# Moving the norm products of a windowed-attention layer from the head of a turn's seventh step to the tail of its sixth

## The chip, the cores and the metric

The kernel runs on one core of a Trainium2 chip. A core has five engines with an instruction queue each: TensorE (PE, matrix products; PEld is its weight load), VectorE (DVE), ScalarE (ACT), GpSimd (POOL) and SyncE (SP, which starts DMAs). The metric is the device time of one execution in microseconds (us), measured from outside the program; the median of several executions is given with the lowest and highest. A profile is one execution recorded by the hardware, and its span can differ from the median by a few microseconds.

## The reference

The program is four layers, one after the other, on two images of 512 channels and 64 x 64 pixels, each layer added to its input after a group norm. The change is in the first layer only, a local attention with a 3 x 3 window and 256 pooled keys:

```python
q = (xf @ W_q + b_q).reshape(B, N, nh, hd).transpose(0, 2, 1, 3)
q_norm = _l2norm(q)
q_scaled = (q_norm + query_embedding[None]) * jax.nn.softplus(temperature)[None]
kv = xf @ W_kv + b_kv
k_l, v_l = (kv[..., :C], kv[..., C:])
k_l = _l2norm(k_l.reshape(B, N, nh, hd)).reshape(B, N, C)
# ... 3 x 3 patches of k_l and v_l, scores against them and against 256 pooled keys,
# ... one softmax over all, and the weighted sums of the values
lt = jnp.einsum('bhnd,hdk->bhnk', q_norm, learnable_tokens) + learnable_bias[None] + a_local
x_local = jnp.einsum('bhnk,bhndk->bhnd', lt, v_local)
x_pool = jnp.einsum('bhnp,bhpd->bhnd', a_pool, v_pool)
out = ((x_local + x_pool).transpose(0, 2, 1, 3).reshape(B, N, C) @ W_proj + b_proj)
```

`_l2norm` divides each head's 64 channels of every pixel by their norm. The change moves the instructions that do this division.

## The kernel before

The first layer works in turns. Each turn handles one unit of 128 channels and 1024 pixels (16 units an image), and several units are in flight at different stages. A stage is a Python generator: it records some instructions, yields, and goes on at its next step. `in_turn` takes one step of every stage in the order of the list, then the next step of every stage, until all have ended:

```python
def in_turn(*gens):
    gens = list(gens)
    while gens:
        gens = [g for g in gens if next(g, gens) is not gens]
```

The turns of an image (`units` is 16; `i` runs over 21 values):

```python
for i in range(-4, units + 1):
    k, q, ahead, u, before = (unit(i + n) for n in (4, 3, 1, 0, -1))
    streams = []
    stages = [self.norms(streams)]
    if before is not None:
        stages.append(self.weigh(before))
    if ahead is not None:
        stages.append(self.tap_products(ahead))
    if u is not None:
        stages.append(self.attend(u))
    if ahead is not None:
        stages.append(self.tap_sums(ahead))
    stages.append(self.projections(k, q, ahead, streams))
    if i < -2:
        stages.append(islice(heads, 12 if i == -4 else None))
    if i == units - 3:
        stages.append(self.fetch_output())
    if i > units - 3:
        stages.append(self.output(i - units + 2))
    in_turn(*stages)
```

`projections` fills `streams` with up to four pieces of raw keys and queries of 512 pixels each; the next turn's `norms` normalises them. Its steps, with numbers added here as comments:

```python
def norms(self, streams):
    before, self.pending = self.pending, streams
    if not before:
        return
    yield                                        # 1: nothing
    ps = self.bank()                             # 2: sums of squares, copied out
    for s in range(4):
        nc.tensor.matmul(ps[32 * s:32 * s + 32, :], self.cst[:, C_E32:C_E32 + 32],
                         before[s % len(before)][4], start=True, stop=True)
    rows = wp.tile([P, TB], F32, name="n_rows")
    nc.scalar.copy(rows, ps)
    yield
    # ... 3: transposed, max with 1e-24 into n; yield
    # ... 4: POOL takes n to the power -1/2, into self.wide; yield
    # ... 5: nothing; yield
    ps = self.bank()                             # 6: transposed back
    for t in range(NT):
        nc.tensor.transpose(ps[:, t * P:(t + 1) * P], self.wide[:, t, :], self.net.ident)
    rows = wp.tile([P, TB], F32, name="n_rows")
    nc.scalar.copy(rows, ps)
    yield
    banks = [self.bank() for _ in before]        # 7: the products
    for s, ps in enumerate(banks):
        nc.tensor.matmul(ps, self.cst[32 * s:32 * s + 2, C_ROW:C_ROW + P],
                         rows[32 * s:32 * s + 2, :], start=True, stop=True)
    for (which, u, j, part, _), ps in zip(before, banks):
        # ... out is the place in kx for a key, part itself for a query
        nc.vector.tensor_tensor(out, part, ps, ALU.mult)
    yield
    if before[-1][0] == "q":                     # 8
        self.learned(before[-1][1])
    yield
```

The other stages at the steps that matter: `weigh` records instructions at its steps 2, 3, 5, 7, 9, 10 and 11 (steps 3, 5, 7 and 9 weigh two of the nine window positions of the values each; step 6 is empty); `tap_products` one DVE product at each of its first nine steps; `attend` the second half's product with the values (`values(1)`) at step 6; `tap_sums` products at steps 3, 5, 7, 9 and 10 and nothing at step 6; `projections` a projection of values at steps 1, 4, 7 and 10, and those of keys and queries at steps 7 to 10, so nothing at step 6. `attend`'s `values`:

```python
def values(j):
    psO = self.bank()
    for k2 in range(2):
        for h, c in enumerate(heads):
            nc.tensor.matmul(psO[c, :], self.vp[:, k2, cc * P + h * HD:][:, :HD],
                             prob[j, k2][h], start=(k2 == 0), stop=(k2 == 1))
    nc.scalar.copy(out[:, j * TB:(j + 1) * TB], psO)
    # ... two sums of prob on POOL
```

`self.bank()` is the next of five PSUM buffers, in rotation, shared by all these stages; the tap products and sums have a buffer apiece of their own.

Of the kernel before, what the change touches and what calls it, by code (L numbers as in the profile page):

```python
# [49 lines left out]
# [6 lines that stand above are left out]
# [872 lines left out]
class Net(General):  # L928
# [361 lines left out]
    def key_context(self, X, Y, d, nmean, rstd, mv, row2, queries, kp, wp, pp):  # L1290
# [19 lines left out]
        def prepare(blk):  # L1310
            ks, sqs = wp.tile([P, KC, TB], F32, name="k"), []
            yield from self.projected_squares(X, wk, bk, blk, ks, sqs, wp, pp)
            if blk == NB - 1:
                queries.wq = self.load3(d, "Wq3")
            ed = wp.tile([P, NT, NH], F32, name="ed")
            va = lent[blk % 2].rearrange("p (t h c) -> p t h c", t=NT, h=NH)
            norms = self.half_norm_columns(sqs, e2h, wp, pp)
            for t in range(NT):
                if t:
                    cols = next(norms)  # L1320
                    if t == 2:
                        nc.scalar.mul(ed.rearrange("p t (c h) -> p t c h", h=2), cols, -1.0)
                lo = blk * TB + t * P
                ps = pp.tile([P, TB], F32, name="mm")
                for kc in range(KC):
                    nc.tensor.matmul(ps, X[:, kc, lo:lo + P], wv[:, kc, :], start=(kc == 0),  # L1326
                                     stop=(kc == KC - 1))
                nc.vector.tensor_tensor(va[:, t].rearrange("p h c -> p (h c)"), ps, row, ALU.add)
                yield
            made[blk] = ks, ed, va  # L1330
            if blk == NB - 1:

                gap = kp.tile([P, KC], F32, name="gap3")
                nc.vector.tensor_tensor(gap, mv[:, :, 0], nmean, ALU.add)
                self.shift_row(vmean, wv, gap, pp)
                queries.wo = self.load3(d, "Wo3")
# [112 lines left out]
class Queries:  # L1449
# [19 lines left out]
    def run(self, dst, fp, pp, ppo, ppd):  # L1469

        nc, ratio = self.nc, fp.tile([P, NH], F32, name="ksum_ratio")
        nc.vector.reciprocal(ratio, self.ksum[:, 0, :])
        nc.vector.tensor_tensor(ratio, ratio, self.ksum[:, 1, :], ALU.mult)
        for blk in range(NB):
            in_turn(self.attend(blk, ratio, dst, fp, pp, ppo, ppd),
                    *([self.prepare(blk + 1, pp)] if blk + 1 < NB else []))
        self.net.at_most(self.tops)
        self.net.at_most(self.lost)

    def prepare(self, blk, pp):  # L1480
# [3 lines left out]
        for _ in net.projected_squares(self.X, self.wq, self.bq, blk, qs, sqs, self.wp, pp):  # L1484
# [8 lines left out]
            yield  # L1493
        norms = net.half_norm_columns(sqs, self.e2h, self.wp, pp)
        next(norms)
        yield
        cols = next(norms)
        src = lost[:, ts].rearrange("p t (c h) -> p t c h", h=2)
        nc.vector.tensor_tensor(src, cols, tops[:, ts].rearrange("p t (c h) -> p t c h", h=2),
# [100 lines left out]
class Local:  # L1600
# [77 lines left out]
    def run(self):  # L1678


        self.nmean, self.rstd, _ = self.net.group_stats(self.X, self.wp, self.pp)
        xs = self.pooled_tokens()
        heads = self.pooled_heads(xs)
        units = KC * self.UN
        unit = lambda u: u if 0 <= u < units else None
        self.pending = []
        for i in "qkv":
            self.fetch(i, 0)
        for i in range(-4, units + 1):
            k, q, ahead, u, before = (unit(i + n) for n in (4, 3, 1, 0, -1))  # L1690
            streams = []
            stages = [self.norms(streams)]
            if before is not None:
                stages.append(self.weigh(before))
            if ahead is not None:
# [3 lines that stand above are left out]
            if ahead is not None:  # L1699
                stages.append(self.tap_sums(ahead))  # L1700
            stages.append(self.projections(k, q, ahead, streams))
            if i < -2:
                stages.append(islice(heads, 12 if i == -4 else None))
            if i == units - 3:
# [4 lines that stand above are left out]
        in_turn(self.output(KC - 1))  # L1709
# [214 lines left out]
                    self.fetch("v", u // self.UN + 1)  # L1924
            yield

    def norms(self, streams):


        nc, wp = self.nc, self.wp  # L1930
# [4 lines that stand above are left out]
        ps = self.bank()  # L1935
# [6 lines that stand above are left out]
        ps = self.bank()  # L1942
        for t in range(NT):
            nc.tensor.transpose(ps[:, t * P:(t + 1) * P], rows[:, t * P:(t + 1) * P],
                                self.net.ident)
        n = wp.tile([P, NT, 4, 2], F32, name="norms")
        nc.vector.tensor_scalar(n, ps.rearrange("p (t s r) -> p t s r", t=NT, s=4)[:, :, :, :2],
                                1e-24, None, ALU.max)
        yield
        nc.gpsimd.tensor_tensor(  # L1950
            self.wide.rearrange("p t (s r) -> p t s r", s=4)[:, :, :, :2], n,
            self.half.rearrange("p (t s h) -> p t s h", t=NT, s=4), ALU.pow)
        yield
        yield
        ps = self.bank()
        for t in range(NT):
            nc.tensor.transpose(ps[:, t * P:(t + 1) * P], self.wide[:, t, :], self.net.ident)
        rows = wp.tile([P, TB], F32, name="n_rows")
        nc.scalar.copy(rows, ps)
        yield  # L1960
        banks = [self.bank() for _ in before]
        for s, ps in enumerate(banks):
            nc.tensor.matmul(ps, self.cst[32 * s:32 * s + 2, C_ROW:C_ROW + P],
                             rows[32 * s:32 * s + 2, :], start=True, stop=True)
        for (which, u, j, part, _), ps in zip(before, banks):
            out = part
            if which == "k":
                y = 1 + u % self.UN * self.UY + j * self.UY // 2
                out = self.kx[:, y:y + self.UY // 2, 1:W + 1]
                part, ps = (a.rearrange("p (y x) -> p y x", x=W) for a in (part, ps))  # L1970
            nc.vector.tensor_tensor(out, part, ps, ALU.mult)
        yield
        if before[-1][0] == "q":
            self.learned(before[-1][1])
        yield
# [324 lines left out]
```

## Time and profile before

| | us |
|---|---|
| median of 3 executions | 5803.81 |
| lowest, highest | 5801.13, 5812.49 |
| span of the profiled execution | 5811.6 |
| PE busy | 5468.7 (94%) |
| DVE busy | 3005.3 (52%) |
| POOL busy | 2109.4 (36%) |
| ACT busy | 1498.8 (26%) |

In the trace a float32 matrix product of 512 columns shows as two passes, so four products are eight rows; transposes show as one. Idle time of an engine stands before the group that it waited to run, with the instruction that ended the wait; "issue" means that the profile shows nothing it waited for. A query by line gives its first and last start: the norms of the first layer, of both images, start between 218.7 us (first sum of squares) and 3915.7 us (last product), with the other layers of the first image between the two groups.

### The profile page before, as it was taken

The numbers are of one execution on the slowest core, as the hardware profiler recorded it, in microseconds if no ns is written. First come the engines' busy times: TensorE is split into PE (matmuls) and PEld (weight loads), VectorE is DVE, ScalarE is ACT, GpSimd is POOL, SyncE is SP. The second block draws the span as 40 slices with busy tenths as digits, with TensorE's granted clock in tenths as the row PEclk, the third lists the DMA queues.
The fourth block names the chain that finished last, engine by engine and source line by source line (L and its number), as shares of the span: only waits on it lengthen the run. The fifth ranks groups of instructions, "written<-read, shape, count | busy, mean of one in ns | idle before, by whom it ended". The sixth has DMA issues, their size and how long they took to land. (4 is left out here: it accounts for less than half of the span.)

```text
span 5811.6 us, 52270 instructions
## 1 busy us (share of the span) xinstructions
PE 5468.7 (94%) x20443; PEld 2358.9 (41%) x20443; DVE 3005.3 (52%) x3344; ACT 1498.8 (26%) x2839; POOL 2109.4 (36%) x1582
## 2 busy tenths in 40 slices
PE   7899999999987899999988999999999788999999
PEld 3333333455333344544343333334553233445443
DVE  3245555644678733444432455556446787334444
ACT  1233332114222233212112333331142122332221
POOL 0145667610320045444401455685103200454343
PEclk9899999999998999999988999999999899999999
DMA  3000000110000000101010000001000000000000
GB/s 137 0 10 15 13 15 26 43 46 8 16 0 0 2 1 1 73 17 35 29 54 0 10 15 17 11 26 58 31 19 5 0 0 2 1 1 15 22 15 23
DMA packets 51572, 118.15 MB, mean 20 GB/s; under 512 B 4786, under 2 KB 17842, under 8 KB 49524
## 3 DMA queue, kind: packets, MB, share of 16 engines
q1 hardware_dynamic: 51316, 114.72, 5.6%
q8 instruction: 163, 2.67, 0.2%
q14 instruction: 93, 0.76, 0.0%
HBM read 74.86 MB, written 39.85 MB: 20 GB/s over the span
## 5 line engine op out<-in xcount | busy, mean ns | idle before, releaser
L133 PE MATMUL mm<-big,w 128*128 128x512 f32 x2560 | 1214.9, 620 | 3.0 <-DVE late L2103 3.0
L2141 POOL TENSOR_TENSOR late<-late,big 128x512 f32<-128x512 f32 x576 | 718.7, 1285 | 378.1 <-DVE big L2136 377.8
L133 PEld LDWEIGHTS mm<-big,w 128*128 128x128 f32 x2560 | 477.0, 196 | 717.7 <-issue 627.6
L1109 PE MATMUL acc<-big,dg 128*128 128x512 f32 x896 | 408.0, 614 | 79.5 <-DVE big L692 51.1
L2136 DVE TENSOR_TENSOR big<-big,mm 128x512 f32<-128x512 f32 x576 | 366.1, 682 | 178.7 <-PE mm L2130 144.1
L1188 POOL TENSOR_TENSOR total<-prob 128x512 f32<-128x512 f32 x128 | 159.7, 1270 | 772.5 <-ACT prob L1185 772.5
L692 DVE TENSOR_TENSOR big<-big 128x3968 f32<-128x3968 f32 x96 | 410.8, 4289 | 38.7 <-PE acc L1109 32.8
L1524 POOL TENSOR_SCALAR qf_sum<-qf,ksum_ratio 128x512 f32<-128x512 f32 x128 | 199.2, 1565 | 549.0 <-ACT qf L1574 351.5
L1361 POOL TENSOR_TENSOR big<-big 128x512 f32<-128x512 f32 x224 | 277.7, 1271 | 235.2 <-ACT big L1352 235.2
L1549 DVE RECIPROCAL k<-psD 128x512 f32<-128x512 f32 x64 | 214.9, 3358 | 187.9 <-PE psD L1546 187.9
L2130 PE MATMUL mm<-late,tapb 18*128 18x512 f32 x1152 | 281.3, 673 | 24.4 <-DVE late L2119 23.4
L1109 PEld LDWEIGHTS acc<-big,dg 128*128 128x128 f32 x896 | 174.0, 197 | 312.1 <-issue 283.2
L2071 POOL TENSOR_TENSOR late<-late 128x512 f32<-128x512 f32 x128 | 160.5, 1279 | 323.3 <-ACT late L2060 306.1
L1286 PE MATMUL mm<-proj,k 64*128 64x256 f32 x2048 | 264.9, 391 | 0.9 <-ACT k L1253 0.9
L1352 ACT ACTIVATE big<-mm,ed 128x256 f32<-128x256 f32 x512 | 194.1, 490 | 276.7 <-DVE top L1348 248.9
L1205 DVE RECIPROCAL recip<-psD 128x512 f32<-128x512 f32 x64 | 214.9, 3358 | 87.1 <-PE psD L1202 87.1
L1491 DVE TENSOR_REDUCE tops<-mm 128x2 f32<-128x512 f32 x256 | 159.4, 682 | 176.5 <-PE mm L1286 176.5
L2011 DVE TENSOR_TENSOR prod<-qs,big 128x1024 f32<-128x1024 f32 x192 | 230.8, 1217 | 35.2 <-PE tap L2024 35.2
L1286 PEld LDWEIGHTS mm<-proj,k 64*128 64x128 f32 x2048 | 207.5, 188 | 94.9 <-issue 78.7
L133 PE MATMUL mm<-big,big 128*128 128x512 f32 x512 | 242.4, 637 | 0.0
L1555 PE MATMUL mm<-k,w 128*128 128x512 f32 x512 | 235.6, 602 | 0.0
L1326 PE MATMUL mm<-w,big 128*128 128x512 f32 x512 | 234.5, 601 | 0.0
(343 smaller groups left out, 7907.7 us busy)
## 6 DMA issues: line engine op xcount, KB each, us to landing
big<-in_x SPq DMA_DIRECT2D x8, 2048.0 KB, 10.6
yd<-late SPq DMA_DIRECT2D x32, 512.0 KB, 2.6
out<-big SPq DMA_DIRECT2D x64, 256.0 KB, 2.0
big<-in_W_kv SPq DMA_DIRECT2D x8, 1024.0 KB, 7.0
big<-yd SPq DMA_DIRECT2D x16, 512.0 KB, 3.6
wd<-big SPq DMA_DIRECT2D x6, 1024.0 KB, 4.8
w<-wd SPq DMA_DIRECT2D x24, 256.0 KB, 3.0
prod<-yd SPq DMA_DIRECT2D x8, 512.0 KB, 4.4
```

Source lines behind the costliest of these rows:

```text
L133: self.nc.tensor.matmul(ps, w[:, kc, :], X[:, kc, blk * TB:(blk + 1) * TB], start=(kc == 0), stop=(kc == KC - 1))
L692: nc.vector.tensor_tensor(o, a, b, ALU.max)
L1109: nc.tensor.matmul(accs[b], dg, src[:, b * TB:(b + 1) * TB], start=(j == 0), stop=(j == 6))
L1205: nc.vector.reciprocal(r, psD)
L1286: nc.tensor.matmul(pS[h][i][:, t, :], k[lo:lo + HD, tok:tok + P], proj[lo:lo + HD, :], start=True, stop=True)
L1326: nc.tensor.matmul(ps, X[:, kc, lo:lo + P], wv[:, kc, :], start=(kc == 0), stop=(kc == KC - 1))
L1361: nc.gpsimd.tensor_tensor(a, a, part, ALU.add)
L1555: nc.tensor.matmul(ps, self.wo[:, kc, oc * P:(oc + 1) * P], qs[:, kc, :], start=(kc == 0), stop=(kc == KC - 1))
L2011: self.nc.vector.tensor_tensor(self.prods[k % 3].rearrange("p (y x) -> p y x", x=W), qs, self.kx[:, y + dy:y + dy + self.UY, dx:dx + W], A ...
L2130: nc.tensor.matmul(ps, self.tapb[32 * q:32 * q + 18, kk, :], el[32 * q:32 * q + 18, :], start=True, stop=True)
L2136: nc.vector.tensor_tensor(dst[:, j * TB:(j + 1) * TB].rearrange("p (y x) -> p y x", x=W), self.vx[:, y:y + self.UY // 2, dx:dx + W], ps.re ...
L2141: nc.gpsimd.tensor_tensor(o, o, dst[:, j * TB:(j + 1) * TB], ALU.add)
```

## The change

The products with the norms, and what follows them, leave `norms` and become a stage of their own, `normed`, which stands in the list after `projections`. It waits out five steps and then does at its sixth step what `norms` did at its seventh. It is meant to bring the products nearer to the copy that feeds them, ahead of the next step's work.

```diff
-            streams = []
-            stages = [self.norms(streams)]
+            streams, ended = [], []
+            stages = [self.norms(streams, ended)]
             if before is not None:
                 stages.append(self.weigh(before))
             # ... tap_products, attend, tap_sums as they were
             stages.append(self.projections(k, q, ahead, streams))
+            stages.append(self.normed(ended))
             if i < -2:
                 stages.append(islice(heads, 12 if i == -4 else None))
             # ...
-    def norms(self, streams):
+    def norms(self, streams, ended):
         # ...
         rows = wp.tile([P, TB], F32, name="n_rows")
         nc.scalar.copy(rows, ps)
-        yield
+        ended += [before, rows]
+        yield
+
+    def normed(self, ended):
+
+        nc = self.nc
+        for _ in range(5):
+            yield
+        if not ended:
+            return
+        before, rows = ended
         banks = [self.bank() for _ in before]
         for s, ps in enumerate(banks):
             # ... unchanged to the end
```

## The prediction

> **What bounds the kernel now.** I read the page's first two parts, then the rows of the products with the norms, who waits around them, and the order in time of one turn. The page first: its busy times and the slices of the span.
>
> ```profile
> PE 5468.7 (94%) x20443; PEld 2358.9 (41%) x20443; DVE 3005.3 (52%) x3344; ACT 1498.8 (26%) x2839; POOL 2109.4 (36%) x1582
> ...
> PE   7899999999987899999988999999999788999999
> ...
> PEclk9899999999998999999988999999999899999999
> ```
>
> TensorE is busy nine tenths of nearly every slice, at nearly full clock, so what the change can win or lose is time on TensorE's queue: matmuls removed (none are) or waits in front of them. Next, the products with the norms, by their line (L1963 in the kernel before):
>
> ```profile
> L1963 PE MATMUL mm<-n_rows,cst x256: 587/692/1218, 230.6 to 3915.7; 2*128 2x512 f32 x128
> ...
>   issue: 22.7, 28
>   ACT n_rows L1959: 9.1, 10
> ...
>   DVE big L1971: 54.0, 32
>   PEld mm L133: 1.7, 2
> ```
>
> There are 256 passes, so 128 products. TensorE waits for the copy that feeds them (L1959) in 10 cases only, 9.1 us together; else for nothing that the profile shows. Last, one turn in the steady part, by the view in order of time (start, length, what, and in brackets the idle time before it and its cause); L1957 are the transposes of the sixth step, L2066 the product of the probabilities with the values, L2130 the next step's weighing:
>
> ```profile
> 648.94 0.66 PE L1957 MATMUL mm<-cst,wide 128*128 128x128 f32 x4
> ...
> 649.53 1.94 PE L2066 MATMUL mm<-late,vp 128*64 128x512 f32 x8
> 649.63 0.59 ACT L1959 COPY n_rows<-mm 128x512 f32<-128x512 f32 x1 [0.93 <-PE mm L1957]
> ...
> 651.39 0.31 PEld L1963 LDWEIGHTS mm<-n_rows,cst 2*128 2x128 f32 x8 [0.81 <-issue]
> 651.39 1.14 PE L1963 MATMUL mm<-n_rows,cst 2*128 2x512 f32 x8
> ...
> 652.36 3.25 PE L2130 MATMUL mm<-late,tapb 18*128 18x512 f32 x8
> 652.55 1.29 DVE L1971 TENSOR_TENSOR big<-big,mm 128x512 f32<-128x512 f32 x2 [0.89 <-PE mm L1963]
> 653.29 0.29 PEld L2130 LDWEIGHTS mm<-late,tapb 18*128 18x128 f32 x2 [0.75 <-DVE big L1971]
> ```
>
> Two things are to be seen here. The copy ends at 649.63 + 0.59 = 650.22, more than a microsecond before the products start at 651.39, because the values' product (1.94 us) lies between: the products come after the last TensorE work of the sixth step already. And the wait that does cost something is behind them: L2130 takes 3.25 us, while in the same turn at 644.92 the same eight passes took 1.14 us, as its banks are free only when VectorE has multiplied the products (L1971).
>
> [...] L1957, L2066, L1963, L2130 start in the order in which they are recorded, and the products don't pass the values' product although their rows were ready at 650.22. So the order of recording is what a move of this kind can change, and the time follows from it. [...] eight passes of 0.59 us or more take 1.14 us together. So the products are 1.14 us a turn, wherever they stand.
>
> **The change part by part.** It removes no instruction and adds none. What it moves, I work out from the lists of stages. In the code before, the products are the first thing recorded in the seventh step, since `norms` heads the list. In the changed code they are recorded in the sixth step by a stage behind `projections`. Between these two places stands only what other stages record after `normed` in step six: the pooled heads, the fetch of the output's weights, and the output. Each of them in turn:
> - The pooled heads have 17 yields. Turn -4 takes twelve, so turn -3 takes the rest; their last work is at its fifth step. At the sixth there is nothing left. Turn -4 has no norms.
> - The fetch of the output's weights (turn 13) waits three steps and records its copies at the fourth. Nothing at the sixth.
> - The output runs in turns 14 to 16. The last queries (unit 15, at i + 3) are projected in turn 12 and normalised in turn 13; from turn 14 on `norms` has nothing to do and `ended` stays empty.
>
> So nothing is jumped over. The second half moves with it: `learned` was at the head of step eight and is now at the tail of step seven, and again none of those three stages records anything between, in a turn that has norms (turn -3's heads ended at step six; the fetch at step five). The rotation of the five PSUM buffers is a count of calls in the same order, so each product gets the bank it had; nor does any call for an `n_rows` buffer move. A turn with nothing pending ends `normed` at its sixth step without an instruction.
>
> The sum is thus: 34 turns with norms (17 an image, -3 to 13), 128 products, each displaced by 0 instructions on TensorE; 128 multiplications on VectorE, 0; 34 copies, 0. The built programs say the same: the queues of all five engines list the same instructions on the same buffers with the same waits, in the same order, and differ in source lines alone. The expected difference is 0 us, before noise.
>
> **The rivals.** Each supposes that the move is real.
> - The products wait for the copy. If they came right behind the transposes, the wait of the 10 cases (9.1 / 10 = 0.91 us) would appear in the other turns too: at most 34 - 10 = 24 of them, 24 x 0.91 = 22 us more, 5826 us. For it speaks that the copy (0.59 us, after 0.93 us of waiting for the transposes) is a chain that TensorE can't overlap with nothing between. Against it: the stage stands behind `attend`, so the 1.94 us of the values' product still lie between.
> - The banks come free sooner. If the products ran before the values' product, VectorE could multiply them 1.94 us sooner and L2130 would fall from 3.25 towards 1.14 us: up to 2.1 us a turn, estimated for 30 full turns at 63 us, less the wait of the first rival (27 us), so some 36 us gained: 5768 us. Against it the same: behind `attend`, nothing starts sooner.
> - The rotation of banks shifts, so that a product waits for another reader. One VectorE multiplication (0.68 us, from 1.29 us for two and an overlap) a turn either way would be 34 x 0.68 = 23 us: 5781 or 5827 us. Against it: the calls keep their order.
> - The first and last turns change, where the stages behind `normed` exist. One turn of them an image has norms as well at each end, four in all, with a TensorE group of 1 to 4 us to be displaced: under 10 us. Against it: they are empty at the steps concerned.
>
> I give all four together about 2 in 100, for a slip in the counting of steps, and even then only the second would be near to 1%, still within the 2%.
>
> **Range and chances.** The predicted time is that of before, 5804 us. The range is only the spread of executions: three of the kernel before lay between 5801.13 and 5812.49, 11.4 us or 0.2% apart, and the profiled span was 5811.6. I take 5798 to 5813: a few microseconds below the lowest, about the highest above; a median of several should lie inside more often than not by a good margin, the rest being left to another chip or another day. A change of over 2% would be 116 us, three times the largest rival, so I give it 1 in 100 on each side.
>
> **What would show it right or wrong.** In the changed kernel's profile the counts of page part one stay as they were (a few records can be missing); the products' row again waits for the copy in about 10 cases, 9 us; a turn in the steady part shows transposes, values' product, products, weighing in this order, with products starting about 2.4 us after the transposes and the weighing again stretched to about 3.25 us behind them; VectorE waits about 54 us for the products in 32 cases. I am wrong if the products stand before the values' product in that view, if the stretched weighing shrinks, or if the medians differ by more than their spreads.

## The result and the profile after

| | median us | lowest to highest |
|---|---|---|
| before | 5806.32 | 5801.13 to 5812.49 (4 executions) |
| after | 5803.80 | 5801.28 to 5812.39 (4 executions) |

The ratio is 0.9998, with a 95% interval of 0.9981 to 1.0015: no difference that can be measured.

The page of the kernel after, its busy times and its clock:

```profile
PE 5461.7 (94%) x20443; PEld 2357.2 (41%) x20443; DVE 3004.3 (52%) x3344; ACT 1497.6 (26%) x2839; POOL 2108.0 (36%) x1582
...
PEclk9899999999999999999988999999999899999999
```

Every count of instructions is the one of before. The products with the norms, now line 1974, in the view by line; the lower lines are what TensorE waited for, and who waited for it:

```profile
L1974 PE MATMUL mm<-n_rows,cst x256: 587/692/1218, 222.7 to 3903.7; 2*128 2x512 f32 x128
...
  issue: 22.7, 28
  ACT n_rows L1960: 9.1, 10
...
  DVE big L1982: 54.0, 32
```

Durations, 28 and 10 waits and their 22.7 and 9.1 us are the same to the last digit; only the starts have shifted. One steady turn in order of time (L1958 transposes, L2077 product with the values, L1974 products with the norms, L2141 weighing of step seven):

```profile
637.50 0.66 PE L1958 MATMUL mm<-cst,wide 128*128 128x128 f32 x4
...
638.08 1.94 PE L2077 MATMUL mm<-late,vp 128*64 128x512 f32 x8
...
639.95 1.14 PE L1974 MATMUL mm<-n_rows,cst 2*128 2x512 f32 x8
...
640.91 3.25 PE L2141 MATMUL mm<-late,tapb 18*128 18x512 f32 x8
```

The order is that of before, the products start 639.95 - 637.50 = 2.45 us behind the transposes as they did (651.39 - 648.94), and the weighing behind them is stretched to 3.25 us again. What holds for this turn holds for the whole trace: the 3344 instructions of VectorE, 2839 of ScalarE and 1582 of GpSimd and the 20443 passes of TensorE come on tiles of the same names in the same order in both profiles.

So the change is without effect because it moves nothing. What was open: is that all, or does the place of the products matter and by what? The experiments start from the changed kernel and move the products for real.

### The profile page after: what moved, and what is told of

Its sections match the earlier page's. It is cut to its first block, busy times and chain, and to the rows that moved or that the text cites. A ratio compares the mean times of both kernels' runs of the same rounds, so it can differ in the third digit from the quotient of the medians.

```text
span 5799.4 us, 52270 instructions
## 1 busy us (share of the span) xinstructions
PE 5461.7 (94%) x20443; PEld 2357.2 (41%) x20443; DVE 3004.3 (52%) x3344; ACT 1497.6 (26%) x2839; POOL 2108.0 (36%) x1582
## 5 line engine op out<-in xcount | busy, mean ns | idle before, releaser
L2141 PE MATMUL mm<-late,tapb 18*128 18x512 f32 x1152 | 280.9, 672 | 21.2 <-DVE late L2130 20.2
```

What stands on the lines that cost most here:

```text
L2141: nc.tensor.matmul(ps, self.tapb[32 * q:32 * q + 18, kk, :], el[32 * q:32 * q + 18, :], start=True, stop=True)
```

## The experiments

Two quantities are used for all runs. A turn's length is the distance between the first copies of the norms in two turns that follow each other. The clock records of the trace say when TensorE was granted half its clock (0.5 in the record, against 1.0); such stretches are counted where they start between 370 and 950 us or between 3270 and 3820 us of the span, where all kernels are in steady turns.

| kernel | median us | ratio to before (95% interval) | steady turns, us | half-clock stretches, us in all |
|---|---|---|---|---|
| before | | | 51.8, 53.4, 54.7 mixed | 19, 112.6 |
| after | 5803.80 | 0.9998 (0.9981 to 1.0015) | 51.8, 53.4, 54.7 mixed | 17, 102.4 |
| again | 5808.82 | 1.0000 (0.9992 to 1.0009) | 51.8, 53.4, 54.7 mixed | 18, 102.4 |
| before_values | 5795.07 | 0.9974 (0.9965 to 0.9984) | 52.0 and 53.7 mixed | 9, 30.7 |
| step_earlier | 5789.44 | 0.9964 (0.9951 to 0.9978) | 52.3 | 0 |
| behind_weigh | 5802.92 | 0.9988 (0.9981 to 0.9994) | 51.8, 53.5, 55.0 mixed | 16, 88.7 |
| before_values_learned8 | 5754.26 | 0.9905 (0.9892 to 0.9918) | 51.5 | 0 |
| step_earlier_learned8 | 5765.57 | 0.9925 (0.9913 to 0.9937) | 51.5, some 53.2 | 5, 17.1 |
| late_start | 5766.28 | 0.9921 (0.9909 to 0.9934) | 51.5, some 53.2 | 5, 17.1 |
| attend_first | 5756.13 | 0.9911 (0.9898 to 0.9924) | 51.5, some 53.2 and 54.8 | 15, 64.9 |
| filler | 5767.83 | 0.9923 (0.9910 to 0.9937) | 51.8 | 0 |
| filler_twice | 5765.84 | 0.9926 (0.9913 to 0.9940) | 51.8 | 0 |
| filler_thin | 5823.59 | 1.0027 (1.0017 to 1.0037) | 54.6 | 21, 136.5 |
| learned8_filler | 5769.49 | 0.9930 (0.9917 to 0.9944) | 51.8 | 0 |

The kernel before had medians of 5808.21, 5810.73 and 5809.48 us in the three groups of runs, in which the first four, the next four and the last four experiments stood. The last group ran on another chip than the first two, so across groups the ratios are compared.

**Again**: the changed kernel, unedited.

> The changed kernel once more, nothing edited, to see how far apart two medians of one and the same program lie. Theory (the change moves no instruction): 5804 us, ratio to the kernel before 1.000, interval containing 1 and about 0.2% wide to each side. Rival (the move of the change does something small, hidden in the spread of the first comparison): a ratio that differs from 1 by 0.1% to 0.3%, in the same direction in most rounds.

1.0000, with an interval of a tenth of a per cent to each side. The first comparison, with a wider one, left room for a small effect; this leaves none over about 0.1%.

**The products ahead of the values' product** (before_values):

```diff
+            stages.append(self.normed(ended))
             if u is not None:
                 stages.append(self.attend(u))
             if ahead is not None:
                 stages.append(self.tap_sums(ahead))
             stages.append(self.projections(k, q, ahead, streams))
-            stages.append(self.normed(ended))
```

> The products really move: ahead of the values' product of the sixth step. Theory (what the products' place costs is the reuse of the banks behind them): the weighing of step seven falls from 3.25 us to about 1.2 us in a steady turn, the products wait 0.9 us more for their copy, net 1.2 us a turn over 30 turns: about 36 us less, 5768 us. Rival (TensorE is full, so a place on its queue is worth nothing and only the new wait shows): 0.9 us in 24 to 30 turns more, 5826 to 5831 us.

A gain, so the rival (a place is worth nothing) is out; but of 0.26%, some 15 us, less than half of the 36. The turn in order of time:

```profile
490.84 1.14 PE L1974 MATMUL mm<-n_rows,cst 2*128 2x512 f32 x8
...
491.91 1.94 PE L2077 MATMUL mm<-late,vp 128*64 128x512 f32 x8
...
493.78 1.88 PE L2141 MATMUL mm<-late,tapb 18*128 18x512 f32 x8
...
496.28 1.60 PE L1995 MATMUL mm<-qn,big 128*32 128x512 f32 x8 [0.62 <-ACT late L2079]
```

The weighing (L2141) fell from 3.25 to 1.88 us, not all the way to the 1.2 that were expected. And the product with the learned tokens (L1995), recorded one step after the products, had moved with them, and TensorE stands idle 0.62 us in front of it, for a bank that ScalarE has still to copy (L2079). The order in which the code records is not always that of the queue, either: one tap sum of step seven (L2035, 1.05 us from 489.86) stands between transposes and products here.

**Transposes and products a step earlier** (step_earlier): `normed` stands right behind `norms`, and one of the two yields after the power is gone.

```diff
             stages = [self.norms(streams, ended)]
+            stages.append(self.normed(ended))
             # ...
-            stages.append(self.normed(ended))
         # norms, after the power:
         yield
-        yield
```

> Transposes one step earlier (fifth), products at the head of the sixth step, so that both the copy and the banks have other work before them. Theory (banks): the weighing of step seven at about 1.2 us instead of 3.25, no wait for the copy, 2.1 us in 30 turns: about 63 us less, 5741 us; less gained if the transposes now wait for POOL's power, which ended about 1.2 us before the fifth step's weighing in the turn looked at. Rival (the place is worth nothing): 5804 us, or more by the wait for POOL.

A gain of 0.36%, some 21 us, a third of the 63 that were expected, and again the learned product stands in the way: TensorE is idle 1.23 us until VectorE has multiplied the queries (L1981).

```profile
483.02 1.65 PE L1994 MATMUL mm<-qn,big 128*32 128x512 f32 x8 [1.23 <-DVE qn L1981]
```

**Products behind the weighing** (behind_weigh): `normed` stands right behind `weigh` and waits six steps.

```diff
                 stages.append(self.weigh(before))
+            stages.append(self.normed(ended))
             # ...
-            stages.append(self.normed(ended))
-        for _ in range(5):
+        for _ in range(6):
             yield
```

> Products one step later, behind the weighing of the seventh step. Theory (banks): eight banks are still wanted in a row of five, so now the products wait for VectorE instead of the weighing: the 2.1 us change hands, 5804 us within 15. Rival (the weighing is what must not be held up, as GpSimd's long sums hang on it): 20 to 60 us less.

The theory holds: 0.12% less than before, within its 15 us and short of the rival's 20. The wait did change hands, in order of time:

```profile
486.91 1.14 PE L2141 MATMUL mm<-late,tapb 18*128 18x512 f32 x8
487.87 3.32 PE L1974 MATMUL mm<-n_rows,cst 2*128 2x512 f32 x8
```

The weighing takes 1.14 us now, and the products, which took 1.14, take 3.32: not 1.14 wherever they stand, as the prediction supposed.

**The learned product back at step eight**, in both kernels that gained (before_values_learned8, step_earlier_learned8):

```diff
             nc.vector.tensor_tensor(out, part, ps, ALU.mult)
         yield
+        yield
         if before[-1][0] == "q":
             self.learned(before[-1][1])
```

> As the run with the products ahead of the values' product (5795 us), but the product with the learned tokens, which had moved with them to step seven, is put back to step eight. Theory (the learned product, 0.62 us idle and 0.5 us stretched behind the last multiplication of the queries, ate half of the gain): 1.2 us in some 26 turns, about 31 us less than that run: 5764 us, and the weighing of step seven stays under 2 us. Rival (VectorE's order is the bound there, so the wait only goes over to the weighing): 5795 us within 6.

> As the run with transposes and products one step earlier (5789 us, turns of 52.3 us), the learned product put back to step eight. Theory: its 1.23 us idle and 0.6 us stretch go, 1.8 us in 24 turns: 43 us less, 5746 us, turns of about 50.5 us, no half-clock windows in the steady part. Rival (the wait goes over to the weighing): 5789 us within 6.

The first went to 5754.26 us, 41 us below its forerunner, where 31 were expected: the best kernel of the study, 0.95% faster than before. The second gained 24 of the 43. In both the learned product was a hindrance, but the 41 us agree with the 31 in part by luck, for they aren't the 1.2 us a turn of the expectation. The sum of the 22 steady turns fell from 1159.4 to 1132.2 us: a turn at full clock by about 0.5 us only (52.0 to 51.5), the rest is that the nine half-clock stretches are gone. The first four turns of both images gave another 12 us. In the second, too, 13 us came from the first four turns; its steady turns are 51.5 us and not 50.5, and five half-clock stretches came back, where none was expected.

But the sum didn't fit. Here is the first one's turn from transposes to weighing:

```profile
523.09 0.66 PE L1958 MATMUL mm<-cst,wide 128*128 128x128 f32 x4
...
523.68 1.05 PE L2036 MATMUL tap<-prod,cst 128*32 128x512 f32 x2
...
524.65 1.14 PE L1974 MATMUL mm<-n_rows,cst 2*128 2x512 f32 x8
...
525.73 1.94 PE L2078 MATMUL mm<-late,vp 128*64 128x512 f32 x8
...
527.59 1.87 PE L2142 MATMUL mm<-late,tapb 18*128 18x512 f32 x8
```

From the start of the transposes to the end of the weighing it takes 527.59 + 1.87 - 523.09 = 6.37 us. In the kernel before it was 652.36 + 3.25 - 648.94 = 6.67 us. The tap sum in between is no added work: the tap sums behind the weighing have two passes less, though they take as long (1.06 us against 1.07). That is 0.3 us a turn, 7 us for 22 steady turns, and the run gained 55. The difference had to be elsewhere, and the lengths of the turns showed where. Three turns of the kernel before in the view by stretches, each from copy to copy (columns: stretch, its length, busy us of PE, PEld, DVE, ACT, POOL with their instructions, mean granted clock of TensorE, DMA share, GB/s):

```profile
633.12:684.88 51.76, 51.76 (x202) 17.22 (x204) 30.22 (x38) 16.66 (x27) 32.65 (x23) 1.00 0.05 16
684.88:738.32 53.44, 53.44 (x202) 17.88 (x204) 30.22 (x38) 16.73 (x28) 32.61 (x23) 0.97 0.06 20
738.32:793.26 54.94, 54.94 (x202) 18.01 (x204) 30.40 (x38) 16.73 (x28) 32.62 (x23) 0.94 0.04 15
```

The instructions are the same, 202 matmul passes each; what differs is the clock. At full clock the turn of before takes 51.76 us, only 0.3 us more than the 51.5 of the best kernel. The longer turns hold one stretch at half clock, by the clock records from 708.3 to 711.7 and from 759.5 to 766.3 us (a mean clock of 0.50 in both). The first starts just as the weighing and the tap sums behind it end, the second within the weighing, and what runs then takes longer (in the turn at full clock the tap sums took 1.07 us, and elsewhere eight passes of a projection take 3.70):

```profile
708.30 5.38 PE L133 MATMUL mm<-big,w 128*128 128x512 f32 x8
...
761.68 1.94 PE L2024 MATMUL tap<-prod,cst 128*32 128x512 f32 x8
```

So the new theory, so far a reading of these turns: the products (two rows) and the weighing behind them (18 rows, its passes one by one as banks come free) are a stretch of 655.61 - 651.39 = 4.2 us in which the array has little to do, and for that TensorE is put at half clock; the values' product (128 rows) between the two breaks the stretch. The sums over the 22 steady turns agree: 1188.7 us before, 1132.2 here. That is 56.5 us, the whole gain; at 51.76 us each the turns of before would take 1138.7, so about 50 us go with the half clock and 6.5 with the waits. The old theory, the wait for banks itself, remains as rival; the last group tells them apart.

**The first turns kept as they were** (late_start): the yields of the kernel before for turns -3 to 0, the new ones from turn 1 on.

```diff
-            stages = [self.norms(streams, ended)]
+            stages = [self.norms(streams, ended, i < 1)]
+            stages.append(self.normed(ended, i < 1))
             # ...
-            stages.append(self.normed(ended))
         # norms, after the power:
         yield
-        yield
+        if late:
+            yield
         # normed:
-        for _ in range(5):
+        for _ in range(6 if late else 5):
             yield
         # ... before the learned product
         yield
+        if not late:
+            yield
```

> The kernel with the learned product back at step eight, but the first four turns of an image keep the old steps. Theory (what the earlier transposes lose is the wait for GpSimd's power in the short first turns, 33.5, 35.0, 36.8, 44.2 us against 31.5, 33.6, 34.1, 41.8 of the kernel before): 8.5 us an image back, about 17 us less than the run beside it: 5729 us. Rival (the first turns wait for something else, as the first attention): 0 to 5 us less.

A miss for the theory: 5766.28 against 5765.57 us, which only the rival's 0 to 5 us fits within noise. The first turns did lose in step_earlier (33.5, 35.0, 36.8, 44.2 us), but with the learned product back at step eight they were at 33.5, 32.2, 34.5 and 42.4 us already: most of that loss, too, was the learned product's and not the wait for GpSimd.

**Attention ahead of the weighing** (attend_first): the same kernel with `attend` before `weigh` in the list.

```diff
+            if u is not None:
+                stages.append(self.attend(u))
             if before is not None:
                 stages.append(self.weigh(before))
             if ahead is not None:
                 stages.append(self.tap_products(ahead))
-            if u is not None:
-                stages.append(self.attend(u))
```

> As late_start, with the attention ahead of the weighing in the list of stages, so that at steps three and five too a product of 1 to 2 us lies between two users of the same banks. Theory (banks behind VectorE are the general cost): the scores of step five fall from 1.6 or 2.0 us to 1.1 and the weighing of step three from 1.77 to 1.1: about 1.2 us in 24 turns, 29 us less than late_start: 5700 us. Rival (the weighing then starts later and GpSimd's sums with it, and TensorE waits for them at the end of the turn): the same time as late_start or up to 30 us more.

Inconclusive: the median is 10 us lower, but the intervals (0.9898 to 0.9924 and 0.9909 to 0.9934) overlap, and the usual turn stays at 51.5 us. So more products between users of the same banks didn't shorten a turn at full clock. Half-clock stretches are more here (15 against 5). In the profiles the 22 steady turns add up to 1152.2 us here and 1144.1 in late_start, so the lower median doesn't come from them; from what is open.

**Work that nobody needs, in the wait** (filler, filler_twice, filler_thin, learned8_filler). In the weighing of step seven, ahead of the first real product and into its bank:

```diff
                     banks[kk, j] = ps = self.bank()
+                    if kk == 4 and j == 0:
+                        for _ in range(1):          # filler_twice: 2
+                            nc.tensor.matmul(ps, self.net.ident,
+                                             self.cst[:, :TB], start=True, stop=True)
+            # filler_thin: self.cst[:2, C_ROW:C_ROW + P] and self.cst[:2, :TB]
+            # learned8_filler: as filler, in before_values_learned8
```

The real product overwrites the filler, so nothing of it reaches the output.

> The changed kernel with one more product that nobody reads: the unit matrix by 512 columns of constants, into the first bank of the weighing of step seven, which the real product overwrites. It adds 0.9 us of dense work to each of 32 turns, in the stretch where TensorE waits for banks. Theory (the cost of the place is the clock: the thin stretch lets TensorE be granted half clock for 3.4 or 6.8 us in most turns, 27 times in the two images): the half-clock windows of the steady turns go, turns of 54.7 us fall to about 52: 40 to 50 us less, 5755 to 5765 us, in spite of the work added. Rival (the cost is the wait for banks itself): no gain, between 5804 us and 0.9 us in 32 turns more, 5833 us.

> Two such products. Theory of the clock: no half-clock windows either, but the second no longer fits into the wait: 0.9 us in 32 turns, about 28 us more than with one, 5785 to 5795 us. Rival (bank wait): 5833 to 5860 us.

> One such product of two rows only (2 by 128, 512 columns), as long as the dense one but on two of the 128 rows of the array. If the clock is granted by time in which TensorE is busy, it does what the dense one does, 5755 to 5765 us; if by how much of the array works, the half-clock windows stay and the time is 5804 us or up to 29 us more. The bank rival expects 5804 to 5833 us as before.

> The dense filler in the kernel with products ahead of the values' product and learned product back at step eight (5754 us), where no half-clock window is left in the steady turns. Theory of the clock: nothing to win, the added product costs what of its 0.9 us the remaining wait of the weighing (1.87 us against 1.14) doesn't hide: 5754 to 5775 us. If it gained here too, by over 10 us, the gain of the filler would be something else than the clock.

The filler makes the kernel 0.77% faster by adding 32 products and taking nothing away. (Its expectation counts 27 half-clock stretches; the profile of before has 24 in the turns of both images.) The dense filler's turn, in order of time (L2143 is the filler):

```profile
429.86 1.14 PE L1974 MATMUL mm<-n_rows,cst 2*128 2x512 f32 x8
430.93 1.13 PE L2143 MATMUL mm<-cst 128*128 128x512 f32 x2
431.99 2.09 PE L2145 MATMUL mm<-late,tapb 18*128 18x512 f32 x8
434.01 1.06 PE L2035 MATMUL tap<-prod,cst 128*32 128x512 f32 x8
435.00 3.70 PE L133 MATMUL mm<-big,w 128*128 128x512 f32 x8
```

and the thin filler's:

```profile
426.83 1.14 PE L1974 MATMUL mm<-n_rows,cst 2*128 2x512 f32 x8
427.79 1.02 PE L2143 MATMUL mm<-cst 2*128 2x512 f32 x2
428.65 3.34 PE L2145 MATMUL mm<-late,tapb 18*128 18x512 f32 x8
431.92 1.94 PE L2035 MATMUL tap<-prod,cst 128*32 128x512 f32 x8
433.79 4.84 PE L133 MATMUL mm<-big,w 128*128 128x512 f32 x8
```

The dense filler fills the wait exactly: 1.13 and 2.09 us where the weighing alone took 3.25. The products still stand directly before the weighing and the wait for their banks is as it was; only the clock has changed: a turn takes 51.8 us, as the turn of before does at full clock (51.76). Behind it the tap sums take 1.06 us against 1.94 and the first projection 3.70 against 4.84: that is half clock in the thin kernel. The view by stretches, of filler and then of filler_thin:

```profile
370.00:950.00 580.00, 580.00 (x2271) 192.00 (x2272) 339.08 (x427) 186.31 (x302) 384.37 (x275) 1.00 0.04 15
```

```profile
370.00:950.00 580.00, 580.00 (x2147) 195.52 (x2146) 325.64 (x407) 177.31 (x286) 356.41 (x255) 0.94 0.04 14
```

Both show TensorE busy all 580 us. One has a clock of 1.00, the other of 0.94. The rival's 5804 to 5833 us fits the thin filler alone and fails for the dense ones. In the kernel with no half-clock stretch the filler wins nothing (0.9930 against 0.9905, the intervals just overlapping), as the theory of the clock wants it. The second filler cost nothing, though about 28 us were expected: the wait was long enough for two. What the two kinds of filler don't tell apart is rows and data: the thin one has fewer rows and other numbers in them.

## Why the prediction was right

- *Nothing is jumped over, in stages or banks*: right. The counts and waits of the products' row are identical, and again at 1.0000 (0.9992 to 1.0009) measures it. The four rivals in which the move is real had no occasion.
- *The first rival, if the products came right behind the transposes they'd wait for the copy*: true in kind. In before_values_learned8 the row waits for the copy in 38 cases, 32.6 us in all, against 10 and 9.1. But the prediction read these as waits of TensorE, and most are of its weight loads: TensorE's own are 4 cases and 2.9 us in the kernels before and after. In the steady turns a tap sum fills the wait, from 523.68 until the products start at 524.65.
- *The second rival, an early place frees the banks, 36 us*: a real place ahead of the values' product is worth more, 55 us, but only with the learned product left where it was (15 us without), and not for that reason. The term "up to 2.1 us a turn" for the stretched weighing was mis-sized: it fell by 3.25 - 1.87 = 1.4 us, and as the wait for the copy (0.97 us here, 0.91 in the prediction) took most of that, 0.3 us a turn are won from transposes to weighing. Nor are there 30 full turns, but 22. The rest was a cost that the prediction didn't see.
- *"At nearly full clock"*: here it lay. The page's clock row shows nines, and a nine stands for 0.9 to 1.0; in the turns it hides 0.94, 0.97 and 1.00, which is three microseconds in a turn of 55. It had no bearing on a change that moves nothing, but would have on one that did.
- *The range, 5798 to 5813*: the medians of after and again lie in it. Single executions of the kernel before reached from 5800.47 to 5822.07 in the later groups, wider than the three I had. The mix of turn lengths is not the main source of this spread. The profiled spans are 5811.6, 5799.4 and 5808.3 us for before, after and again; their first-layer turns add up to 1567.8, 1565.9 and 1563.1, and 219.8, 211.9 and 217.7 us pass before the first copy of norms. So 8 of the 12 us between before and after lie ahead of that copy, where nothing differs; why is open.

Left open: why the turn ends at 51.5 us at full clock however the waits are spread; and what in the work decides when TensorE is granted half its clock.

## What to carry to other kernels

Where code is recorded by generators in turns, work out what stands between the old and the new place before costing a move: the end of one step and the head of the next are the same place when the stages between them are empty there, and what was recorded behind the moved piece moves too (the learned product cost 41 us of a gain of 55, 12 of them in the short first turns). When TensorE is busy all the time and a stage is still longer than its twin, look at the granted clock stretch by stretch: a dense product put between two thin ones, even a useless one in a wait, was worth more here than the wait itself (in the steady turns about 50 us by the clock, against 6.5 us of waits that the best real move won).

## What the runs showed of the hardware

Half clock came without idle time that the profile shows. In the kernel before TensorE shows as busy for all of a turn of 54.94 us, at a mean clock of 0.94, while step_earlier, in whose turn TensorE is idle for 1.23 us in one piece, has no half-clock stretch in its steady turns (mean clock 1.00 from 370 to 950 us and from 3270 to 3820 us). Time in matrix products doesn't set the two single fillers apart: one of 2 rows, 1.02 us long, left 21 stretches (mean clock 0.94 in both spans), one of 128 rows, 1.13 us long, none (1.00). How much of the array works fits both fillers; which part of it counts, rows or data, these runs don't show. In the steady turns of before 5 of the 19 stretches last 3.4 us and 14 last 6.8. Those that start at 489.8, 544.4 and 599.1 us are 54.6 us apart, one in each of three turns of 54.73, 54.67 and 54.63 us; whether the stretches hold the turns at that length or the turns place the stretches, no run shows. With the dense filler a steady turn takes 51.8 us and none holds half clock.
